# Half of the first feed-forward pair's first matrix moved into the last four attention steps

## The chip, the cores and the metric

The kernel runs on one core of a Trainium2 chip. The metric is the device time of one execution in microseconds (us), lower is better. Five engines work side by side, each with its own instructions in a fixed order: TensorE (PE: matmuls; PEld is its loading of weights), VectorE (DVE), ScalarE (ACT), GpSimd (POOL), and SyncE (SP), which here issues nearly all DMA transfers. An engine goes to its next instruction only when the one before has been released by the semaphores that it waits for, so a waiting instruction holds up everything behind it on its engine. The profile also shows the clock that was granted to TensorE, as a share of full speed (PEclk).

## The reference

One layer on 16 sequences of 128 queries of width 512, all in fp32, in three parts. Each adds its result to its input `x`:

```python
x = x + cross_attention(layernorm(x), ctx)   # 16 heads of 32, context of 2048 positions for each sequence
x = x + mamba_block(layernorm(x))
x = x + ffn(layernorm(x))                    # shared matrix + two gated experts' share, width 512 to 512

def mamba_block(Z):
    x, z = split(Z @ in_proj.T)                          # 2 x 1024 channels
    x = silu(causal_conv(x))                             # four taps along the 128 positions
    dt, B, C = split(x @ x_proj.T)
    h[t] = exp(dt * A) * h[t-1] + dt * B * x             # 16 states for each channel: the scan
    y = (sum_n h[t] * C + x * D) * silu(z)
    Zm = rmsnorm(y @ out_proj.T + Z) * norm1_w
    h1 = gelu(Zm @ w1.T + b1)                            # 512 -> 2048
    return rmsnorm(h1 @ w2.T + b2 + Zm) * norm1_w        # 2048 -> 512
```

The change bears on `Zm` and on `h1` of the first two sequences.

## The kernel before

**Attention.** The loop `for u in range(last)` near line 1160 is the backbone. For u from 0 to NU − 1 = 255 it is an attention step: one sequence, one block of 512 context positions, one group of four heads. A step goes on PE as `scores(u)` (L302, four matmuls into the four PSUM banks), `weighted(u-1)` (L346, the values of the step before, into the PSUM tile `avp`), and `turn(u, i)` (L333, 16 transposes of the exponentials). Between scores and turn lie `maxima(u)` on DVE (L310, four reductions of the banks) and `exps(u)` on ACT (L320, four exponentials). `turn` copies its banks to the tiles `pT` on ACT (L338), one in four on DVE (L336). PE also makes keys and values from the context in these steps (L240), as products of sums of blocks with prepared factors of the weights: tiles `ka..` and `ks..` hold those for the keys. That work, `y_products` and `x_products`, uses the PSUM tiles `pa` and `pc`. Its last part is in step 252. In steps 253 to 255 PE has attention alone, and in step 256 only `weighted(255)`.

**Mamba.** The sequences form 8 groups of two. Group g runs behind attention: its scans, step r of 32, lie in step u = 54 + 32g + r. `decays` (L664, ACT) write exp(dt·A) of four of 16 states into a state buffer in PSUM, one half (i = 0, 1) after the other, `scan` (L678, DVE) runs the recurrence in place, L681 multiplies with C, and POOL adds up (L694). `inputs` (L643, POOL) prepare the next step's right side `w`. The rows `bc` with B and C are loaded by SP (L592) for every step, two loads of 512 KB, each of which waits for the instruction that last read its buffer. The state buffer is `hst`; for the second half, `states` (L651) names `pc` instead from step NU − 2 = 254 on, when `pc` is no longer needed for keys and values. `anew` sets the first position of a state buffer to zero (a memset, L657).

**Feed-forward.** Pairs of sequences m = 0 to 7, 256 tokens each: `z_norm(m)` is the RMS norm of two sequences (a root in small steps on DVE and ACT, lines 73 to 91, then two products of 128 × 512, L806), `turned_in` and `turned_pair` turn the rows (L813, L834) into a tile `mT`, `hidden(m, q)` multiplies with a quarter q of `w1` (L842: four chunks of 128 columns, each four matmuls over 256 tokens, which the profile counts as 32 instructions a quarter), `gelus(m, q)` (L856) writes `hs` with a table load of ACT before and one after, `second(m, q)` multiplies with a quarter of `w2` (L873), and further units hold the experts and the sums. A quarter of `w1` or `w2` is loaded by `load_wf` into two tiles `wf` of 512 KB (six buffers).

**The order.** It is written out by hand. Dictionaries (`late`, `after`, `inner`, `middle`, `loads`, `head`, `behind`) put functions at places inside a step u: `loads` at its start, `middle` after the second scan, `late` after that on PE (transposes and projections, each given a PSUM bank), `inner` near its end. From step NU + 1 = 257 on, the list `units` of the feed-forward part is fed into the steps evenly: `feeds * (u - NU) // (last - 1 - NU)` units up to step u, with last = 314. `feed(k)` issues the loads of unit k + 2, PE's work of unit k, and what comes after unit k − 1. At u = NU the attention pool is closed, PSUM banks go to a free list, and `open_ffn` opens the feed-forward pool, turns the pair's copies into `mT`, loads `b1` and the first two quarters of `w1`. For pair 0, the rows come by `load_z(0)` in step 251, `z_norm(0)` in step 253, its transposes in step 255.

Of the kernel before, what the change touches and what calls it, by code (L numbers as in the profile page):

```python
# [15 lines left out]
P = 128  # L16
# [18 lines left out]
def perceiver_layer(ctx: ExitStack, tc: tile.TileContext, a: dict, out: bass.AP):  # L35
# [73 lines left out]
    with ExitStack() as es:  # L109
# [8 lines left out]
        def acon_in(name, shape, src=None):  # L118
            t = acon.tile(shape, FP, tag=name, name=name)
            nc.gpsimd.dma_start(t, a[name] if src is None else src)  # L120
            return t
# [364 lines left out]
        dtb = acon_in("dtb", [P, EC])  # L486
        dskip = acon_in("dskip", [P, EC])
        aneg = acon_in("alog", [P, EC, DS])

        zTs, xas, zss, bcs, dts, wts, ysum, wts_in = ({} for _ in range(8))  # L490
        sgs = []
# [158 lines left out]

        def states(g, r, i):  # L651

            return pc if i and 32 * (g + 1) + LAG + r >= NU - 2 else hst

        def anew(h):

# [71 lines left out]
        def open_ffn():  # L728
            p = es.enter_context(tc.tile_pool(name="ffn", bufs=1))
            fpool.append(p)  # L730

            def put_in(name, src, shape):
                t = p.tile(shape, FP, tag=name, name=name)
                nc.sync.dma_start(t, src)
                fcs[name] = t

            turned_pair(0)
            load_wf(0, 1, 0)
            put_in("b1", a["b1"], [P, FC])
            load_wf(0, 1, 1)  # L740

        def load_rows():
            for name in ("b2", "fbias"):
# [57 lines left out]
        def z_norm(m):  # L801
# [3 lines left out]
            for i, b in seqs(m):  # L805
                nc.vector.scalar_tensor_tensor(  # L806
                    xrs[b], xrs[b], r[:, i : i + 1], fcs["normw"], ALU.mult, ALU.mult
                )

        def turned_in(src, b, key, ps=None):  # L810
            ps = bank() if ps is None else ps
            for kc in range(KC):
                nc.tensor.transpose(heads(ps)[:, kc, :], src[:, kc * P : (kc + 1) * P], ident)  # L813
            stage[b, key] = ps
# [22 lines left out]
        def hidden(m, q):  # L837
            ps = [bank(), bank()]
            for j in range(4):
                w = wfs[m, 1, q, j // 2]  # L840
                for kc in range(KC):
                    nc.tensor.matmul(  # L842
                        ps[j // 2][:, j % 2 * MT : (j % 2 + 1) * MT],
                        w[:, kc, j % 2 * P : (j % 2 + 1) * P],
                        mTs[m][:, kc, :],
                        start=(kc == 0),
                        stop=(kc == KC - 1),
                    )
            stage[m, q] = ps

        def gelus(m, q):
            ps = stage.pop((m, q))
            t = fpool[0].tile([P, 4, MT], FP, tag="hs", name=f"hs{m}_{q}", bufs=4)
            for j in range(4):
                fc = q * 4 + j
                nc.scalar.activation(  # L856
                    t[:, j, :],
                    ps[j // 2][:, j % 2 * MT : (j % 2 + 1) * MT],
                    AF.Gelu,
                    bias=fcs["b1"][:, fc : fc + 1],  # L860
                )
            nc.scalar.preload_act_table_set("natural_log_exp_and_others")
            give_back(*ps)
            hss[m, q] = t

        def second(m, q):
            if q == 0:
                accs[m] = [bank(), bank()]
            order = [(j, i) for j in range(4) for i in range(MB)]
            if q == 3:  # L870
                order.sort(key=lambda ji: ji[1])
            for j, i in order:
                nc.tensor.matmul(  # L873
                    accs[m][i],
                    hss[m, q][:, j, i * NQ : (i + 1) * NQ],
                    wfs[m, 2, q, j // 2][:, j % 2, :],
                    start=(q == 0 and j == 0),
                    stop=(q == 3 and j == 3),
                )
# [129 lines left out]
        both = tuple(range(MB))  # L1009

        def hidden_units(m):
            for q in range(4):
                unit([call(load_wf, m, 1, q)], [call(hidden, m, q)], [call(gelus, m, q)])
            if m:
                units[-4][2].append(call(mlp_norm, m - 1, both))
                units[-3][2].append(call(last_norm, m - 1, both))
                units[-1][1].insert(0, call(x_turned, m - 1, both))
# [58 lines left out]
            )  # L1076


        late, after, inner, middle, loads, head, behind = ({} for _ in range(7))

        def put(where, u, f):
            where.setdefault(u, []).append(f)
# [45 lines left out]

        for b in range(1, B):
            put(late, 16 * b - 6, lambda ps, b=b: turned(b, ps))  # L1130
        put(inner, NU - 3, lambda: anew(pc))
        put(loads, NU - 20, load_normw)
        put(loads, NU - 5, lambda: load_z(0))
        put(inner, NU - 3, lambda: z_norm(0))
        for i, b in seqs(0):
            put(late, NU - 1, lambda ps, b=b: turned_in(xrs[b], b, "mT", ps))


        ways = (("k", pa, pc, "u2"), ("v", halves(banks[0]), halves(banks[1]), "u2v"))
# [56 lines left out]
        for u in range(last):  # L1196
            live = u < NU
            g, r = divmod(u - 32 - LAG, 32)
            scans = 0 <= g < NG

            made, phase = divmod(u + 3, 4)
            makes = 0 < made < B * SB
            of, phase = ("k", "v")[phase // 2], phase % 2
            load_bc(u + 2 - 32 - LAG, 0)
            if u % 4 == 1 and made + 1 < B * SB:
                load_ctx(made + 1, ("c00", "c10", "c11"))
            if u % 4 == 2 and made + 1 < B * SB:
                load_ctx(made + 1, ("c01",))
            for f in loads.get(u, ()):
                f()  # L1210
            if scans:
                decays(g, r, 0)
            if u > NU:
                while fed < feeds * (u - NU) // (last - 1 - NU):
                    feed(fed)
                    fed += 1
            load_bc(u + 1 - 32 - LAG, DS)
            if u == NU + 1:
                load_rows()
            if live:  # L1220
                scores(u)
            if 1 <= u <= NU:
                weighted(u - 1)
            if u == NU:
                att.close()
                give_back(flat(pa), banks[2], banks[1], flat(avp))
                open_ffn()
            if u == NU + 8:
                load_wex()
            for f in head.get(u, ()):  # L1230
                f()
            if live:
                maxima(u)
            if makes:
                x_products(of, made, phase, pa, pc)
            if live:
                exps(u)
            if makes and u % 4 == 1:
                ctx_sums(made, ("t1", "t2"))
            if 0 <= u + 1 - 32 - LAG < 32 * NG:  # L1240
                inputs(*divmod(u + 1 - 32 - LAG, 32))
            if makes and u % 4 == 1:
                ctx_sums(made, ("t3", "t4"))
            silu_third()
            if scans:
                scan(g, r, 0)
            if makes:
                hold(of, made, pa, "u1")
            if scans:
                decays(g, r, 1)  # L1250
            if makes:
                x_sums(of, made, phase, pa, pc)

            after_turns = late.get(u, ())
            places = [banks[(3 + i) % 4] for i in range(len(after_turns))]
            if live and after_turns:
                if u % 4 == 0:
                    places = [flat(avp), *places[:-1]]  # L1260
                elif u % 2 and makes and u not in behind:
                    places[-1] = flat(pc)
            taken = sum(any(p is b for b in banks) for p in places)
            if live:
                for i in range(3 if taken else 4):
                    turn(u, i, i)
            if scans:
                scan(g, r, 1)
            for f in middle.get(u, ()):
# [99 lines left out]
```

## Time and profile before

| | us |
|---|---|
| median of three runs | 3802.73 |
| lowest and highest run | 3801.78, 3805.72 |
| the profiled execution's own time | 3809.03 |
| its span, from the first to the last instruction | 3807.2 |
| PE busy in the span | 3747.0 |
| DVE, ACT, POOL busy | 2690.4, 2443.9, 2107.1 |
| `scores` of steps 252, 253, 254, 255 begin at | 3069.46, 3080.39, 3087.69, 3101.64 |
| `weighted(255)`, first `hidden`, first `second` begin at | 3111.93, 3118.39, 3151.33 |

Busy time of an engine is the union of its instructions; idle time of one that isn't the bound costs nothing. In a timeline row the first number is the start, the second the length of a run of equal instructions, and the bracket says how long the engine stood idle before it and which instruction ended that by the record of semaphores. A wait for several semaphores is put down to the last. Times inside the execution are from the start of its span.

### The profile page before, as it was taken

What the parts mean: (1) busy time and instruction counts of PE and PEld (TensorE: products, weight loads), DVE (VectorE), ACT (ScalarE), POOL (GpSimd) and SP (SyncE); (2) the same over time, 40 slices, a digit from 0 to 9 for tenths busy, and PEclk for the clock granted to TensorE, in tenths of its full rate; (3) what the DMA queues carried; (4) which work ended last, traced back from release to release, by engine and by line L of the source; (5) the groups of instructions that cost most, each with busy time, mean ns of one, the idle gap of its engine ahead of it and who ended that gap; (6) DMA issues with size and microseconds to landing.
All of it is one profiled execution on the core that took longest, in us unless ns stands there. A gap on an engine that the chain in (4) does not pass through costs nothing.

```text
span 3807.2 us, 70317 instructions
## 1 busy us (share of the span) xinstructions
PE 3747.0 (98%) x26120; PEld 2858.7 (75%) x26120; DVE 2690.4 (71%) x4852; ACT 2443.9 (64%) x5847; POOL 2107.1 (55%) x1968
## 2 busy tenths in 40 slices
PE   8999999999999999999999999999999989999999
PEld 7878787778777877787778878787878766655555
DVE  3444445887878777877787778877887777767843
ACT  3555556777767776777677767776777665545421
POOL 2111213675667665766676566666676667567730
PEclk9999999999999999999999999999999989999999
DMA  3111122444444435353534353445344457577752
GB/s 101 34 40 43 55 65 79 136 154 139 137 162 141 156 120 176 129 166 118 175 131 156 116 187 128 148 134 178 131 148 136 159 186 263 191 256 257 263 194 72
DMA packets 341223, 548.40 MB, mean 144 GB/s; under 512 B 24432, under 2 KB 225408, under 8 KB 340624
## 3 DMA queue, kind: packets, MB, share of 16 engines
q1 hardware_dynamic: 340464, 543.28, 43.2%
q8 instruction: 206, 3.38, 0.4%
q14 instruction: 137, 1.12, 0.1%
q0 software_dynamic: 416, 0.63, 0.1%
HBM read 527.29 MB, written 16.52 MB: 143 GB/s over the span
## 4 chain that ended last, share of the span: by engine, by line
PE 90%; DVE 5%; ACT 3%; issue 1%; POOL 1%; DMA 1%; SPq 0%; DVEq 0%; POOLq 0%; ACTq 0%
PE pa L240 24%; PE pc L240 17%; PE bank L333 11%; PE bank L302 7%; PE avp L346 6%; PE bank L526 4%; PE bank L873 3%; PE bank L968 2%; PE bank L842 2%; PE bank L472 2%; PE avp L399 1%; PE bank L707 1%; PE pc L707 1%; PE pa L873 1%; PE pc L526 1%
## 5 line engine op out<-in xcount | busy, mean ns | idle before, releaser
L310 DVE TENSOR_REDUCE nm<-bank 128x1 f32<-128x512 f32 x1024 | 635.3, 682 | 250.2 <-PE bank L302 250.0
L694 POOL TENSOR_TENSOR ysum<-ysum,w 128x512 f32<-128x512 f32 x384 | 500.7, 1304 | 487.7 <-DVE hst L657 305.8
L320 ACT ACTIVATE pr<-bank,nm 128x512 f32<-128x512 f32 x1024 | 689.8, 687 | 101.0 <-DVE nm L310 97.0
L643 POOL TENSOR_TENSOR w<-dx,bc 128x512 f32<-128x512 f32 x512 | 653.0, 1296 | 4.7
L678 DVE TENSOR_TENSOR_SCAN hst<-hst,w 128x512 f32<-128x512 f32 x456 | 557.0, 1221 | 12.8 <-ACT hst L664 8.5
L338 ACT COPY pT<-bank 128x512 f32<-128x512 f32 x816 | 434.9, 585 | 183.2 <-PE bank L333 179.4
L333 PE MATMUL bank<-ident,pr 128*128 128x128 f32 x4096 | 517.5, 274 | 14.4 <-ACT pr L320 10.5
L664 ACT ACTIVATE hst<-dt,alog 128x254 f32<-128x254 f32 x912 | 436.5, 479 | 145.5 <-DVE hst L657 126.1
L333 PEld LDWEIGHTS bank<-ident,pr 128*128 128x128 f32 x4096 | 471.4, 142 | 66.1 <-ACT pr L320 17.0
L346 PEld LDWEIGHTS avp<-pT,v 128*32 128x32 f32 x8192 | 208.6, 110 | 195.0 <-issue 177.4
L681 DVE TENSOR_TENSOR w<-hst,bc 128x512 f32<-128x512 f32 x456 | 315.2, 691 | 21.2 <-DMA bc<-bcd 5.7
L232 POOL TENSOR_TENSOR t<-c,c 128x512 f32<-128x512 f32 x128 | 164.4, 1285 | 259.4 <-PE pc L240 253.2
L302 PE MATMUL bank<-kt,qT 32*128 32x512 f32 x2048 | 301.3, 643 | 0.9 <-ACT pT L338 0.9
L346 PE MATMUL avp<-pT,v 128*32 128x128 f32 x8192 | 277.6, 276 | 0.0
L240 PE MATMUL pa<-t,ks 128*128 128x256 f32 x1024 | 249.8, 387 | 6.1 <-POOL t L232 6.1
L240 PE MATMUL pa<-vs,t 128*128 128x256 f32 x1008 | 244.7, 386 | 0.0
L240 PEld LDWEIGHTS pa<-t,ks 128*128 128x128 f32 x1024 | 184.8, 190 | 44.2 <-issue 10.6
L240 PEld LDWEIGHTS pa<-vs,t 128*128 128x128 f32 x1008 | 185.4, 190 | 34.6 <-issue 10.1
L320 ACT ACTIVATION_READ_ACCUMULATOR pr<-bank,nm 128x1 f32 x1024 | 209.9, 205 | 0.0
L336 DVE COPY pT<-bank 128x512 f32<-128x512 f32 x208 | 143.8, 691 | 89.6 <-PE bank L333 88.1
L232 POOL TENSOR_TENSOR t<-c,t 128x512 f32<-128x512 f32 x128 | 163.4, 1276 | 36.5 <-issue 19.6
L526 PE MATMUL bank<-zT,win 128*128 128x256 f32 x792 | 182.7, 381 | 0.0
(319 smaller groups left out, 6890.4 us busy)
## 6 DMA issues: line engine op xcount, KB each, us to landing
bc<-bcd SPq DMA_DIRECT2D x512, 512.0 KB, 4.3
c<-in_ctxT_dram SPq DMA_DIRECT2D x256, 256.0 KB, 4.3
wf<-in_w_dram SPq DMA_DIRECT2D x128, 512.0 KB, 7.0
wqo<-in_wqkvo_dram SPq DMA_DIRECT2D x128, 256.0 KB, 4.9
win<-in_win_dram SPq DMA_DIRECT2D x128, 256.0 KB, 4.5
wout<-in_wout_dram SPq DMA_DIRECT2D x128, 256.0 KB, 4.0
x<-in_x_dram SPq DMA_DIRECT2D x16, 256.0 KB, 4.3
x1d<-x SPq DMA_DIRECT2D x16, 256.0 KB, 2.1
```

Of the source, the lines that this page charges most:

```text
L240: nc.tensor.matmul(ps[:, r, :], l[:, kc, r * P : (r + 1) * P], m[:, kc, :], start=(i in (1, 2, 5) and r == 0 and kc == 0), stop=(r == 1 an ...
L302: nc.tensor.matmul(banks[j], qts[b][rows, hg, :], kts[u // 4, hg][rows, :], start=True, stop=True)
L310: nc.vector.tensor_reduce(stats[b][0][j][:, sb, hg : hg + 1], banks[j], AX.X, ALU.max, negate=True)
L320: nc.scalar.activation(pr[:, j, :], banks[j], AF.Exp, bias=nm[j][:, sb, hg : hg + 1], accum_out=sm[:, sb, h : h + 1],)
L333: nc.tensor.transpose(ps[:, j, :], prs[u][:, j, i * P : (i + 1) * P], ident)
L338: nc.scalar.copy(pT, ps)
L346: nc.tensor.matmul(avp[j * HD : (j + 1) * HD, hg, :], vts[u // 4, hg // 2, i // 2][:, i % 2, hg % 2 * P + j * HD : hg % 2 * P + (j + 1) * HD],
L526: nc.tensor.matmul(ps, w[:, kc, :], zTs[g][:, kc, :], start=(kc == 0), stop=(kc == KC - 1))
L643: nc.gpsimd.tensor_tensor(w, dx.unsqueeze(1).to_broadcast([P, NH // 2, GT]), bcs[g * 32 + r, 0][:, i * NH // 2 : (i + 1) * NH // 2, :], AL ...
L664: nc.scalar.activation(bt(h[:, k, :])[:, :, 1:], bt(dt)[:, :, 1:], AF.Exp, scale=aneg[:, ec, n : n + 1],)
L678: nc.vector.tensor_tensor_scan(flat, flat, w.rearrange("p n t -> p (n t)"), 0.0, ALU.mult, ALU.add)
L694: nc.gpsimd.tensor_tensor(s, s, w, ALU.add)
```

## The change

- `b1` is loaded at the start, by the queue of the other constants, not in `open_ffn`.
- The rows of pair 0 are loaded in step 249, not 251. Their norm is cut into `early_first` (step 248), `early_second` and `early_third` (249), and `early_norm` of each sequence (250, 251). `early_turned` transposes both in step 252, and copies them in halves into two tiles of the tag `ws`, which Mamba's weights use.
- The first half of `w1`, quarters 0 and 1, is loaded in eight chunks of 256 KB: four in step 251 into the tiles of factors of keys that are no longer used, four in step 252 into tiles of the tag `ws`.
- `early_hidden` multiplies two chunks in each of steps 253 to 256, in `pa`, `pc`, `pa`, `pc`, between `weighted(u-1)` and the turns of the step. `early_gelus` follow at the end of steps 254 and 256, into tiles of the tag `zs`.
- As `pa` and `pc` are taken, `states` gives `pc` to the second half only from step 257 on, and its first memset is in step 256.
- `hidden_units(0)` has two units, not four; `open_ffn` loads quarters 2 and 3. The feed of units into steps 257 to 313 is spread over 65 units, not 67. `hss` holds four separate tiles or slices for each quarter.

```diff
-            return pc if i and 32 * (g + 1) + LAG + r >= NU - 2 else hst
+            return pc if i and 32 * (g + 1) + LAG + r > NU else hst
...
-            turned_pair(0)
-            load_wf(0, 1, 0)
-            put_in("b1", a["b1"], [P, FC])
-            load_wf(0, 1, 1)
+            load_wf(0, 1, 2)
+            load_wf(0, 1, 3)
...
+        def early_first():
+            ms, r = small("ms", [P, MB]), small("rz", [P, MB])
+            mean_square(keep, ms, mvz[:, 0:MB, :])
+            stage["early"] = r, *root_first(keep, ms, 1e-6)
+
+        def early_second():
+            root_second(*stage["early"][1:])
+
+        def early_third():
+            root_third(*stage["early"])
+
+        def early_norm(i):
+            x = xrs[i]
+            nc.vector.scalar_tensor_tensor(
+                x, x, stage["early"][0][:, i : i + 1], fcs["normw"], ALU.mult, ALU.mult
+            )
+
+        def early_turned(i, ps):
...
+            for kc in range(KC):
+                nc.tensor.transpose(heads(ps)[:, kc, :], xrs[i][:, kc * P : (kc + 1) * P], ident)
+            for h in range(2):
+                copy = nc.vector.tensor_copy if i else nc.scalar.copy
+                copy(mTs[0][h][:, :, i * NQ : (i + 1) * NQ], heads(ps)[:, 2 * h : 2 * h + 2, :])
+
+        def load_early(c):
+            if c < 4:
+                tag = ("ka11", "ka12", "ks3", "ka22")[c]
+                t = pool.tile([P, 2, 256], FP, tag=tag, name=f"w1_{c}", bufs=1)
+                t = t.rearrange("p a b -> p (a b)").rearrange("p (k o) -> p k o", o=P)
+            else:
+                t = ssm.tile([P, KC, P], FP, tag="ws", name=f"w1_{c}", bufs=WS)
+            nc.sync.dma_start(t, a["w1"][c // 4][:, :, c % 4 * P : (c % 4 + 1) * P])
+            wfs["early", c] = t
+
+        def early_hidden(c):
+            ps = (pa, pc)[c // 2 % 2][:, c % 2, :]
+            for kc in range(KC):
+                nc.tensor.matmul(
+                    ps,
+                    wfs["early", c][:, kc, :],
+                    mTs[0][kc // 2][:, kc % 2, :],
+                    start=(kc == 0),
+                    stop=(kc == KC - 1),
+                )
+
+        def early_gelus(q):
+            hss[0, q] = [ssm.tile([P, GT], FP, tag="zs", name=f"hs0_{q}_{j}", bufs=16) for j in range(4)]
+            for j in range(4):
...
+                    (pa, pc)[j // 2][:, j % 2, :],
+                    AF.Gelu,
+                    bias=b1[:, fc : fc + 1],
...
+            nc.scalar.preload_act_table_set("natural_log_exp_and_others")
...
-            for q in range(4):
+            for q in range(0 if m else 2, 4):
...
-        put(inner, NU - 3, lambda: anew(pc))
-        put(loads, NU - 5, lambda: load_z(0))
-        put(inner, NU - 3, lambda: z_norm(0))
-        for i, b in seqs(0):
-            put(late, NU - 1, lambda ps, b=b: turned_in(xrs[b], b, "mT", ps))
+        put(loads, NU - 7, lambda: load_z(0))
+        put(inner, NU - 8, early_first)
+        put(middle, NU - 7, early_second)
+        put(inner, NU - 7, early_third)
+        for i in range(MB):
+            put(inner, NU - 6 + i, lambda i=i: early_norm(i))
+            put(late, NU - 4, lambda ps, i=i: early_turned(i, ps))
+        for c in range(8):
+            put(loads, NU - 5 + c // 4, lambda c=c: load_early(c))
+            put(early, NU - 3 + c // 2, lambda c=c: early_hidden(c))
+        put(inner, NU - 2, lambda: early_gelus(0))
+        put(inner, NU, lambda: early_gelus(1))
+        put(inner, NU, lambda: anew(pc))
+        put(inner, NU, lambda: give_back(flat(pa)))
...
-                give_back(flat(pa), banks[2], banks[1], flat(avp))
+                give_back(*banks, flat(avp))
                 open_ffn()
+            for f in early.get(u, ()):
+                f()
```

More of the change, by code (lines that the diff above doesn't have):

```diff
@@ L488, in perceiver_layer @@
         aneg = acon_in("alog", [P, EC, DS])
+        b1 = acon_in("b1", [P, FC])
         zTs, xas, zss, bcs, dts, wts, ysum, wts_in = ({} for _ in range(8))
@@ L730, in open_ffn @@
             fpool.append(p)
[L732 to L735, printed above, removed]
-            turned_pair(0)
-            load_wf(0, 1, 0)
-            put_in("b1", a["b1"], [P, FC])
-            load_wf(0, 1, 1)
+            load_wf(0, 1, 2)
+            load_wf(0, 1, 3)
         def load_rows():
@@ new lines, in early_turned @@
+        def early_turned(i, ps):
+            if i == 0:
+                mTs[0] = [
+                    ssm.tile([P, KC, P], FP, tag="ws", name=f"mT0_{h}", bufs=WS).rearrange(
+                        "p a b -> p (a b)"
+                    ).rearrange("p (k t) -> p k t", t=MT)
+                    for h in range(2)
+                ]
+            for kc in range(KC):
[3 more added lines that the diff above has]
+                copy(mTs[0][h][:, :, i * NQ : (i + 1) * NQ], heads(ps)[:, 2 * h : 2 * h + 2, :])
@@ L810, in turned_in @@
+        def early_gelus(q):
+            hss[0, q] = [ssm.tile([P, GT], FP, tag="zs", name=f"hs0_{q}_{j}", bufs=16) for j in range(4)]
+            for j in range(4):
+                fc = q * 4 + j
+                nc.scalar.activation(
+                    hss[0, q][j],
+                    (pa, pc)[j // 2][:, j % 2, :],
+                    AF.Gelu,
+                    bias=b1[:, fc : fc + 1],
+                )
+            nc.scalar.preload_act_table_set("natural_log_exp_and_others")
         def turned_in(src, b, key, ps=None):
@@ L844, in hidden @@
                         w[:, kc, j % 2 * P : (j % 2 + 1) * P],
-                        mTs[m][:, kc, :],
+                        mTs[m][:, kc, :] if m else mTs[m][kc // 2][:, kc % 2, :],
                         start=(kc == 0),
@@ L859, in gelus @@
                     AF.Gelu,
-                    bias=fcs["b1"][:, fc : fc + 1],
+                    bias=b1[:, fc : fc + 1],
                 )
@@ L863, in gelus @@
             give_back(*ps)
-            hss[m, q] = t
+            hss[m, q] = [t[:, j, :] for j in range(4)]
         def second(m, q):
@@ L874, in second @@
                     accs[m][i],
-                    hss[m, q][:, j, i * NQ : (i + 1) * NQ],
+                    hss[m, q][j][:, i * NQ : (i + 1) * NQ],
                     wfs[m, 2, q, j // 2][:, j % 2, :],
@@ L1076, in perceiver_layer @@
             )
+        early = {}
         late, after, inner, middle, loads, head, behind = ({} for _ in range(7))
```

## The prediction

> **What bounds the kernel now.** First the page's rows of busy time and of granted clock, and its chain of the work that ended last:
>
> ```profile
> PE 3747.0 (98%) x26120; PEld 2858.7 (75%) x26120; DVE 2690.4 (71%) x4852; ACT 2443.9 (64%) x5847; POOL 2107.1 (55%) x1968
> ...
> PEclk9999999999999999999999999999999989999999
> ...
> PE 90%; DVE 5%; ACT 3%; issue 1%; POOL 1%; DMA 1%; SPq 0%; DVEq 0%; POOLq 0%; ACTq 0%
> ```
>
> TensorE (PE) is busy 98% of 3807.2 us, so most of the kernel gains nothing from a freer VectorE (DVE) or ScalarE (ACT). But one digit of the clock row is an 8, where attention hands over to the feed-forward part: the place of the change. So second the stretches from step 253 on (columns: window, its length, busy time and count of PE, PEld, DVE, ACT, POOL, then granted clock, DMA share, GB/s). The cuts are the starts of steps 253, 254, 255, of `weighted(255)`, and of the first `hidden` matmul:
>
> ```profile
> 3080.39:3087.69 7.30, 4.79 (x58) 2.95 (x57) 5.55 (x9) 5.75 (x15) 6.27 (x7) 1.00 0.31 118
> 3087.69:3101.64 13.95, 7.49 (x57) 4.87 (x57) 11.70 (x24) 7.17 (x19) 6.78 (x6) 0.72 0.25 88
> 3101.64:3111.93 10.29, 10.13 (x67) 7.20 (x66) 8.57 (x14) 6.49 (x16) 5.03 (x4) 0.55 0.30 104
> 3111.93:3118.39 6.46, 1.08 (x33) 0.84 (x33) 5.96 (x12) 5.04 (x12) 5.27 (x5) 0.95 0.70 219
> 3118.39:3125.00 6.61, 6.61 (x17) 5.30 (x18) 6.31 (x13) 3.18 (x6) 5.50 (x7) 0.53 1.07 364
> 3125.00:3150.00 25.00, 25.00 (x119) 21.98 (x118) 13.20 (x22) 18.50 (x35) 21.18 (x22) 1.00 1.03 389
> ```
>
> Read PE's time against the length: from 3080.39 to 3118.39 it works 23.5 of 38 us, and part of that at half clock. After 3125 it is full again, with DMA nearly full too. Third, PE's timeline names the gaps (start, length, instruction; in brackets the idle time before it and who ended it):
>
> ```profile
> 3096.67 0.47 PE L333 MATMUL bank<-ident,pr 128*128 128x128 f32 x1 [5.88 <-ACT pr L320]
> ...
> 3109.29 1.85 PE L813 MATMUL bank<-ident,xr 128*128 128x128 f32 x8
> ...
> 3118.39 6.75 PE L842 MATMUL pa<-mT,wf 128*128 128x256 f32 x16 [5.38 <-ACT hst L664]
> 3124.98 7.07 PE L842 MATMUL bank<-mT,wf 128*128 128x256 f32 x32
> ```
>
> The 5.88 us wait for `exps(254)`. Behind it stands the order of DVE, from its timeline and SP's:
>
> ```profile
> 3092.35 2.85 DVE L806 SCALAR_TENSOR_TENSOR xr<-xr,rz,normw 128x512 f32<-128x512 f32 x2
> 3095.12 2.47 DVE L310 TENSOR_REDUCE nm<-bank 128x1 f32<-128x512 f32 x4
> ...
> 3113.12 1.23 SPq L774 DMA_DIRECT2D wf<-in_w_dram  x2
> ```
>
> `z_norm(0)`, 3089.22 to 3095.2 on DVE, sits ahead of `maxima(254)`, whose scores were ready by 3089.8. The 5.38 us are put down to an ACT instruction that writes no operand of the matmul. I take the weights as the releaser: issued at 3113.12, and their tile's fastest landing in this stretch is 5.1 us, hence 3118.2. Sixteen hidden instructions then take 6.75 us where the next 32 take 7.07 (3.46 for 16): 3.3 us lost to the clock.
>
> **The change, part by part.** I follow PE from 3080.39 to the end of `hidden` of pair 0. In the profile that is 3150.02, less 0.87 for six small instructions of lines 459 and 610 in between (3142.25 to 3143.12): 3149.15, or 68.8 us.
>
> *Norm in parts.* The 6.0 us of DVE leave step 253. `early_first` is 0.27+0.27+0.90 = 1.4 us, `early_third` 1.25, the two products 1.43 each, now in steps 248 to 251. There PE is full (steps 250 to 252 take 10.9, 9.6 and 10.9 us with no bracket on PE, DVE 9.2 of 10.9 busy in step 252), and the products with key and value factors hide them; without that cover they would cost their 5.5 us. Value 0; the stall it removes is counted below.
>
> *Transposes.* The eight of line 813 leave step 255 (1.85 us at half clock) and go to step 252 at 0.88 us (8 × 0.11, as in the row of L333). The four half copies on ACT and DVE fall under the factor products of step 252. So step 253 starts at 3081.3.
>
> *Early matmuls.* Eight chunks of four matmuls, which the profile counts as 64 instructions: 64 × 0.216 (7.07 us for 32, by their spacing 6.91) = 13.8 us, two chunks (3.46 us) in each of steps 253 to 256, between `weighted(u-1)` and `turn(u)`. Step by step, at full clock (scores 1.07, weighted 1.07, turn 16 × 0.11 = 1.75):
> - 253: scores and weighted to 3083.4, chunks 0, 1 to 3086.9; `exps(253)` are done by then (they ended near 3085 in the trace), turn to 3088.6.
> - 254: scores to 3089.7, weighted to 3090.8, chunks 2, 3 to 3094.2, turn to 3096.1. `maxima` and `exps` (2.5 and 2.8 us) lie under the chunks.
> - 255: the first scores wait some 0.9 us for a copy as they do at 3087.69, to 3098.4; weighted to 3099.4; chunks 4, 5 wait about 0.9 for `early_gelus(0)` to free `pa`, to 3103.7; turn waits for `exps(255)`.
> - Those `exps` stand behind `early_gelus(0)` on ACT: a table load of 1.28, four of 0.42, a load of 1.28, 4.2 us. By ACT's order they run 3103.3 to 3106.0, so turn ends at 3107.6, line 610 at 3108.1, `weighted(255)` at 3109.2. In the trace it ended at 3113.0.
> - 256: chunks 6, 7 to 3112.65.
>
> *`states`.* Both halves of the scans of 254 to 256 use one buffer, so `decays` of the second half wait for the first scan: 0.7 to 1 us on ACT in each, as in all steps up to 253 today. It is inside the ACT order above; alone it could cost 0 to 3 us. `anew(pc)`, a memset of 0.06 us, moves to 256.
>
> *What is left of `hidden`.* q = 2 and 3. Their tiles wait for the attention pool, for a copy of step 255, and on SP behind a `bc` load that waits for the second scan of 255 (about 3109.8): issued near 3110.3, landing 5.1 us later, 3115.4. PE waits 2.75 us. Then 64 instructions, 13.8 us: 3129.2. If the tile takes the 7.3 us that is the median of these loads in 3108 to 3165, the wait is 4.95.
>
> *Eight added loads* of 256 KB in steps 251 and 252, in a stretch at 0.31 of DMA's share; 4.3 us is what loads of that size take, and 10 us pass before use. On SP two of them wait for factor products of step 250. Behind them is queued a `bc` load that then goes out near 3060.4 and is used near 3074: slack of 9 us after landing. `b1` at the start, 8 KB: nothing.
>
> Sum: 3149.15 − 3129.2 = 19.95 us. Its parts: 3.8 from `weighted(255)` ending earlier although 10.4 us of hidden work now stand before it; 2.6 less wait for weights (5.38 to 2.75); 3.3 of clock; 13.8 hidden matmuls that no longer follow; less 3.45 for chunks 6, 7 before the wait. That is 20.05, within rounding.
>
> *After it.* From 3118 on PE waits for only some 26 us in 690, so a lead of PE reaches the end as far as the others keep pace. DVE has 42.97 of 50 us in 3450 to 3500, and the pace rises by 20/690 = 3%: enough. (The loop now spreads 65 units over the same steps, not 67; each step still holds some 8 us of PE units.) But at some points PE comes close to others: `second(0, 0)` needs `w2` tiles that are issued by step, the adds of POOL at 3153.9 (line 467), `wex`. I take off 2 us for such waits (bounds 0 and 8): **18 us**.
>
> Two rules bear on this. First, the row: ACT's gelu load starts at 3123.98 after an instruction that ended at 3123.96, and lasts 1.28; no other gap stands around it. The Trainium skill, "ScalarE: Activation LUTs", section "What ACT_TABLE_LOAD costs", puts 1.38 us of drain on top of each switch: 2.66 in all. By it `early_gelus(0)` would hold ACT for 7.0 us, and `exps(255)` end 2.8 us later: gain 15. The row decides, 18. Second, the clock: the gaps of 5.88 and 5.38 us were each followed by 0.5. "TensorE: Matmul & The Clock Gate", Part 1, names an idle window of about 3.4 us. My wait of 2.75 lies below it, so the clock stays at 1.0; at 4.95 it would not, and the gain falls by 2.2+3.3 to 12.5. The trace has no gap between 0.93 and 5.38 here, so the edge is the page's.
>
> **Rivals.**
> *It pays less (gain 4 to 12, about 3795).* The weights land late and the clock drops (−5.5), and the one-buffer scans and gelus each push ACT by 2 to 3 us. For it: DMA moves 364 to 389 GB/s after 3118, its share 1.03 and above. Against it: two of the four MB of `w1` are in before.
> *Slower.* The loads of `w2` stay tied to the steps while PE is 20 us ahead. In the trace they go out from 3133.56 for use at 3151.33; now use is at 3130. I get 3.5 MB ahead of and with the first, 3110.3 + 9.5 + 2 = 3122, and 7 MB up to the second, 3131 for use at 3137: slack of 6. If each of the four units found its tile over 3.4 us late, each costs that and 3.3 of clock: 4 × 6.7 = 27 us, 9 over the gain, **3812**. Up to 2.7 us late it remains a gain of 7 or more.
> *More (gain 24 to 28).* SP frees earlier, so that the wait for weights vanishes (2.75), and two waits of the tail, 4.6 us for ACT ahead of line 526 and 3.4 for POOL ahead of line 580, close as PE's other work falls differently beside them: 3774 to 3779.
> *It doesn't do it:* the early matmuls could merely lengthen the attention steps by their own 13.8 us, as they would if scores and copies, not `exps`, paced them. Then only the norm's stall is won, about 5 us: 3798, part of the first rival.
>
> **How the numbers follow.** The runs' median is 3802.73, the profiled execution 3809.03 with a span of 3807.2; the sum uses differences inside that span, which I take off the median: 3802.73 − 18 = **3785**. Chances: this 0.58 (own range 3780 to 3791), less 0.19, more 0.13, giving the gain back 0.10, of which 0.07 ends slower. A difference under 0.2% (7.6 us: 3795.1 and 3810.3) can't be told from none. Half of the "less" case lies beyond it: faster 0.58 + 0.13 + 0.09 = 0.80; same 0.10 + 0.03 = 0.13; slower 0.07. For 8 in 10 the range drops the slower case and the far end of "more": 3773 to 3801.
>
> **What would show it.** Right: the waits of PE in steps 253 to 256 sum to under 6 us, granted clock 1.00 from step 254 on, `weighted(255)` ends near 3109, the first matmul of q = 2 is preceded by 2 to 3 us, `second(0, 0)` starts near 3130, and PE's idle time after it stays near 26 us. Wrong: a wait over 3.4 us and clock near 0.5 in 254 to 257 (ACT's gelus or weights), or new waits of `second` for `wf` after 3130, or PE's lead at 3130 present but gone in the tail.

## The result and the profile after

The changed kernel takes 3791.64 us (six runs, 3787.74 to 3794.15) where the kernel before takes 3804.77 beside it (six runs, 3801.78 to 3806.85): ratio 0.9959, 95% interval 0.9949 to 0.9969, so 12 to 19 us less; the two medians lie 13.1 us apart. Two later sets gave 0.9958 and 0.9955. Forecast were 18 us less.

From the page of the changed kernel, the rows of busy time, of granted clock and of the chain that ended last:

```profile
PE 3742.2 (99%) x26120; PEld 2853.8 (75%) x26120; DVE 2689.9 (71%) x4853; ACT 2443.5 (64%) x5848; POOL 2109.4 (56%) x1969
...
PEclk9999999999999999999999999999999999999999
...
PE 89%; DVE 5%; ACT 3%; DMA 1%; issue 1%; POOL 1%; SPq 0%; DVEq 0%; POOLq 0%; ACTq 0%
```

The 8 in the clock row is gone. The stretches that answer to those of before (same columns): steps 253, 254 and 255, `weighted(255)` with chunks 6 and 7, the wait for weights, and the first 3 us of `hidden`:

```profile
3081.84:3089.32 7.48, 7.48 (x74) 5.89 (x73) 4.64 (x8) 5.93 (x15) 5.16 (x5) 1.00 0.24 83
3089.32:3098.17 8.85, 8.31 (x73) 6.64 (x73) 7.50 (x13) 6.29 (x17) 5.93 (x6) 1.00 0.20 61
3098.17:3109.71 11.54, 10.08 (x75) 6.77 (x75) 7.49 (x12) 11.04 (x23) 5.04 (x4) 1.00 0.39 136
3109.71:3114.44 4.73, 4.73 (x49) 3.76 (x48) 4.62 (x10) 2.36 (x5) 3.41 (x4) 1.00 0.46 131
3114.44:3116.93 2.49, 0.00 (x0) 0.03 (x1) 1.25 (x3) 2.02 (x4) 1.92 (x2) 0.97 0.93 310
3116.93:3120.00 3.07, 3.07 (x7) 2.49 (x8) 2.58 (x7) 3.04 (x6) 1.96 (x2) 0.50 1.08 383
```

Steps 253 to 255 keep the full clock, and step 254 is 8.85 us where it was 13.95, with 3.46 us of hidden work in it. But step 255 is 11.54, longer than the 10.29 of before, with ACT busy 11.04 of it. And the wait for weights is still followed by half clock. PE's timeline at the hand-over:

```profile
3101.29 3.72 PE L851 MATMUL pa<-mT,w 128*128 128x256 f32 x16
...
3110.72 3.72 PE L851 MATMUL pc<-mT,w 128*128 128x256 f32 x16
3116.93 15.65 PE L903 MATMUL bank<-mT,wf 128*128 128x256 f32 x64 [2.50 <-DMA wf<-in_w_dram]
3132.42 1.02 PE L934 MATMUL avp<-wf,hs 128*128 128x512 f32 x2
```

The wait of 2.50 us is now put down to the load itself, as was read from the issue time before. The 64 hidden instructions take 15.49 us to the next start; at full clock they would take 13.8.

What one execution can tell: the start of the program alone moves the span by up to 4 us. `scores(250)` begin between 3045.64 and 3049.63 us in the traces of the runs. The clock granted in the first 60 us differs too: in executions of the kernel before, of the changed kernel and of the run `e1_norm` below it was (window row, same columns; PEclk is the third number from the end):

```profile
0.00:60.00 60.00, 50.18 (x256) 39.67 (x257) 22.91 (x42) 17.91 (x42) 18.46 (x25) 0.94 0.45 138
```

```profile
0.00:60.00 60.00, 52.49 (x255) 40.74 (x256) 21.56 (x42) 17.98 (x42) 18.56 (x26) 0.91 0.43 138
```

```profile
0.00:60.00 60.00, 51.59 (x300) 39.95 (x300) 23.07 (x44) 18.82 (x44) 19.00 (x26) 1.00 0.43 138
```

The changed kernel's own three executions have 0.91, 0.97 and 0.97, so the change is not what sets it. `scores(250)` begin at 3048.88, 3049.15 and 3045.93 in the three above. The parts of the norm in steps 248 and 249 lie before that point, but the kernel before and the changed one go through these two steps in 27.44 and 27.45 us. So profiles are compared here from `scores(250)` to the end of the span. For the kernel before that is 3807.2 − 3048.88 = 758.3 us. For the changed kernel, profiled three times, it is 742.9, 743.9 and 745.3: 15.5, 14.5 and 13.0 less. So this measure too is good only to some 2 us.

### The profile page after: what moved, and what is told of

Its sections match the earlier page's. It is cut to its first block, busy times and chain, and to the rows that moved or that the text cites. A ratio compares the mean times of both kernels' runs of the same rounds, so it can differ in the third digit from the quotient of the medians.

```text
span 3792.0 us, 70325 instructions
## 1 busy us (share of the span) xinstructions
PE 3742.2 (99%) x26120; PEld 2853.8 (75%) x26120; DVE 2689.9 (71%) x4853; ACT 2443.5 (64%) x5848; POOL 2109.4 (56%) x1969
## 4 chain that ended last, share of the span: by engine, by line
PE 89%; DVE 5%; ACT 3%; DMA 1%; issue 1%; POOL 1%; SPq 0%; DVEq 0%; POOLq 0%; ACTq 0%
PE pa L240 24%; PE pc L240 17%; PE bank L333 11%; PE bank L302 7%; PE avp L346 6%; PE bank L527 5%; PE bank L1029 2%; PE bank L934 2%; PE bank L472 2%; PE bank L708 2%; PE bank L903 1%; PE avp L399 1%; PE pc L708 1%; PE avp L934 1%; PE pa L934 1%
## 5 line engine op out<-in xcount | busy, mean ns | idle before, releaser
L679 DVE TENSOR_TENSOR_SCAN hst<-hst,w 128x512 f32<-128x512 f32 x459 | 560.7, 1222 | 15.8 <-ACT hst L665 9.3
L333 PEld LDWEIGHTS bank<-ident,pr 128*128 128x128 f32 x4096 | 469.6, 141 | 57.5 <-issue 13.8
L682 DVE TENSOR_TENSOR w<-hst,bc 128x512 f32<-128x512 f32 x459 | 317.4, 692 | 26.0 <-DMA bc<-bcd 10.4
```

The costliest lines, as they stand in the source:

```text
L333: nc.tensor.transpose(ps[:, j, :], prs[u][:, j, i * P : (i + 1) * P], ident)
L679: nc.vector.tensor_tensor_scan(flat, flat, w.rearrange("p n t -> p (n t)"), 0.0, ALU.mult, ALU.add)
```

## The experiments

Ratios are to the kernel before, run beside each. The "lead" is how much earlier than in the kernel before the first `second` matmul starts, counted from `scores(250)`. The 2.18 us of small matmuls of lines 459 and 610 that stand ahead of it in the kernel before are taken off where a run has them behind it.

| run | ratio, interval | lead, us | `scores(250)` to end, us | less than before, us |
|---|---|---|---|---|
| changed kernel | 0.9959 (0.9949 to 0.9969) | 17.0 | 742.9 | 15.5 |
| `e1_norm` | 0.9968 (0.9955 to 0.9980) | 7.2 | 748.7 | 9.6 |
| `e2_load` | 0.9957 (0.9945 to 0.9970) | 14.5 | 743.2 | 15.1 |
| `e3_states` | 0.9994 (0.9986 to 1.0002) | 1.0 | 759.4 | −1.1 |
| `e5_q2`, `r_e5` | 0.9952 (0.9939 to 0.9964), 0.9951 (0.9938 to 0.9965) | 21.3, 21.3 | 740.8, 745.8 | 17.5, 12.5 |
| `r_after`, `r_after2` | 0.9958 (0.9945 to 0.9970), 0.9955 (0.9942 to 0.9967) | 16.6, 18.1 | 743.9, 745.3 | 14.5, 13.0 |
| `e6_fill` | 0.9961 (0.9947 to 0.9974) | 18.3 | 742.6 | 15.8 |
| `e7_steps` | 0.9965 (0.9952 to 0.9977) | 14.8 | 743.8 | 14.5 |
| `e8_clock` | 0.9991 (0.9983 to 1.0000) | 5.0 | 753.5 | 4.8 |

### The norm alone

From the changed kernel, the early matmuls and their loads are taken out again:

```diff
-            return pc if i and 32 * (g + 1) + LAG + r > NU else hst
+            return pc if i and 32 * (g + 1) + LAG + r >= NU - 2 else hst
-        for c in range(8):
-            put(loads, NU - 5 + c // 4, lambda c=c: load_early(c))
-            put(early, NU - 3 + c // 2, lambda c=c: early_hidden(c))
-        put(inner, NU - 2, lambda: early_gelus(0))
-        put(inner, NU, lambda: early_gelus(1))
-            for q in range(0 if m else 2, 4):
+            for q in range(4):
```

> This has only the norm in parts, its transposes in step 252 and the copies in halves; all four quarters of hidden stay behind attention, weights loaded as before. Theory (the norm's place in VectorE's order made the 5.88 us gap, and the half clock after it): steps 253 to 255 take about 7.5 us each, weighted(255) ends near 3105 instead of 3113, the wait for the first weights stays over 5 us with half clock after it; 8 us faster than before, ratio 0.998. Rival (the gap is filled by other waits of the exponentials, and most of the change's 15 us comes from the matmuls put into gaps): 2 to 4 us faster, ratio 0.999 to 0.9995.

Measured: 0.9968, and 9.6 us by the profile. Its PE timeline:

```profile
3085.91 2.09 PE L302 MATMUL bank<-kt,qT 32*128 32x512 f32 x8 [0.93 <-ACT pT L338]
...
3093.16 2.10 PE L302 MATMUL bank<-kt,qT 32*128 32x512 f32 x8
...
3109.63 5.35 PE L903 MATMUL pa<-mT,wf 128*128 128x256 f32 x16 [5.89 <-DMA wf<-in_w_dram]
```

Step 254 is 7.25 us (3085.91 to 3093.16), not 13.95: the gap of 5.88 is gone, and no other took its place. The wait for weights stays, at 5.89, with half clock after it. The theory holds: 9.6 of the 13 to 15.5 us at the end are there with 6 us of VectorE work moved out of the way of four reductions. (The eight transposes left step 255 with it, so their share is in this number.)

### The weights early, the matmuls behind attention

To `e1_norm`, the eight chunks are loaded in steps 252 and 253 (four into two context tags kept in a pool of their own, four into `ws`), and `hidden(0, 0)` and `hidden(0, 1)` use them as ordinary units after attention:

```diff
+        for c in range(8):
+            put(loads, NU - (3 if c < 4 else 4), lambda c=c: load_early(c))
...
-                w = wfs[m, 1, q, j // 2]
+                early = m == 0 and q < 2
+                w = wfs["early", 4 * q + j] if early else wfs[m, 1, q, j // 2]
```

> As the run with the norm alone, and the first half of w1 is loaded in steps 252 and 253, but its matmuls follow attention, none lies in an attention step. Theory (weights at hand remove the 5.4 us wait and the half clock behind it; filling gaps brings only about 1 us on balance, since the changed kernel has a wait of 2.5 us and half clock before q = 2 again): first hidden matmul within 1 us of weighted(255)'s end, clock 1.00, end of hidden near 3133; 15 us faster than before, ratio 0.996, as the changed kernel. Rival (filling the gaps is what pays): no better than the norm alone plus 3, so 5 to 11 us faster.

Measured: 0.9957, 15.1 us by the profile; the changed kernel, which has half of those matmuls in attention's steps, has 13.0 to 15.5. Its first hidden matmul follows `weighted(255)` at once:

```profile
3101.74 1.08 PE L348 MATMUL avp<-pT,v 128*32 128x128 f32 x32
3102.75 3.72 PE L908 MATMUL pa<-mT,w 128*128 128x256 f32 x16
```

So the weights' early arrival is worth the rest, and the place of the matmuls nothing that can be seen at the end. A part of the reason is in the lengths of steps 253, 254 and 255 of this run, against 7.48, 8.85 and 11.54 in the changed kernel:

```profile
3078.53:3085.83 7.30, 4.78 (x58) 2.94 (x57) 5.55 (x9) 5.75 (x15) 5.16 (x5) 1.00 0.37 128
3085.83:3093.27 7.44, 6.05 (x56) 3.75 (x56) 6.47 (x13) 6.56 (x17) 5.59 (x6) 0.94 0.20 73
3093.27:3101.74 8.47, 7.93 (x59) 4.94 (x59) 7.67 (x13) 6.77 (x17) 5.35 (x5) 0.65 0.52 183
```

In the changed kernel the chunks, with the gelus and the one-buffer scans that came with them, lengthen the three steps by 0.2, 1.4 and 3.1 us: 4.7 of the chunks' own 10.4. Of the 5.7 won, 2.5 go to the wait for weights, which this run doesn't have, and 1.7 to the half clock behind it. With nothing but chunks 6 and 7 between `weighted(255)` and quarter 2, the loads that wait for attention's end have lost their cover. `e2_load` in turn loses about 1 us, most of it in a wait of 0.93 us for POOL within `hidden`. So the matmuls in the gaps do bring some 2.5 us, the difference of the two leads, 17.0 and 14.5. At the end it is gone: the other part of the reason lies behind the hand-over, and `e6_fill` below shows it.

### One buffer for the scans

```diff
-            return pc if i and 32 * (g + 1) + LAG + r >= NU - 2 else hst
+            return pc if i and 32 * (g + 1) + LAG + r > NU else hst
...
-        put(inner, NU - 3, lambda: anew(pc))
+        put(inner, NU, lambda: anew(pc))
```

> The kernel before with one edit: both halves of the scans of steps 254 to 256 use one buffer. Theory (decays then wait for the first half's scan, as in all steps up to 253): 0 to 2 us slower, ratio 1.000 to 1.0005. Rival (the second buffer had hidden more): 3 to 6 us slower.

Measured: 0.9994, interval 0.9986 to 1.0002, and 1.1 us more by the profile. No cost of 3 us or more; the first answer stands.

### Filling the idle time with matmuls that nobody reads

Three runs put matmuls of identity by the norm's weights, 128 x 512, into PE's gaps, to see what the half clock costs by itself:

```diff
+        def idle_fill(n, ps):
+            for i in range(n):
+                nc.tensor.matmul(ps, ident, fcs["normw"], start=True, stop=True)
...
+            if u in (NU - 2, NU):
+                idle_fill(6, flat(pa))
```

The first is the kernel before with six of them behind `weighted` in steps 254 and 256, as in the diff:

> The kernel before, with six matmuls that nothing reads (5.2 us) in each of its two long gaps: before the turns of step 254, and before the first hidden matmul. Nothing is moved. Theory (of the time before, some 7 us are not the waits themselves but the half clock after each): turns of 254 at full speed (1.5 us), step 255 some 2.5 to 3 us shorter, the first 16 hidden instructions 3.3 us shorter, sum 6 to 8 us faster, ratio 0.998. Rival (PE at half clock was still ahead of the exponentials, so only the hidden matmuls gain): 3 to 4 us.

Measured: 0.9991 (0 to 6.5 us), 4.8 by the profile. The clock stayed at 1.00 from 3078 to 3124, while the exponentials and the weights came no earlier. The first hidden instructions after the filled gap:

```profile
3108.07 5.42 PE L1081 MATMUL pa<-normw,ident 128*128 128x512 f32 x12
3114.50 3.69 PE L842 MATMUL pa<-mT,wf 128*128 128x256 f32 x16 [1.01 <-ACT pc L664]
```

3.69 us where it was 6.75, as expected. Step 254 fell from 13.95 to 12.77 us (3085.70 to 3098.47) and 255 from 10.29 to 8.59. Together 1.2 + 1.7 + 3.1 = 6.0; but the first `hidden` matmul came 7.44 us after the start of `weighted(255)`, not 6.46, which leaves 5.0 at this place, and 4.8 at the end. It lies between the two expectations: in the attention steps the exponentials hide a part of the half clock.

The same in the changed kernel, three matmuls at the hand-over:

```diff
+            if u == NU:
+                idle_fill(3, banks[0])
```

> The changed kernel with three matmuls added that nothing reads (identity by the norm's weights, 128 x 512, some 2.6 us in all) in the 2.5 us in which PE waits for the tile of quarter 2. Theory (the wait, though only 2.5 us long, makes the clock fall to half for 3.2 us): the first 16 hidden instructions take 3.5 us and not 5.1, granted clock 1.00 throughout, 1.6 us faster than the changed kernel. Rival (the half clock comes from the crowded DMA or the reload of work after the hand-over, not from idle time): half clock stays, no gain, or 0.1 us lost.

```profile
3110.77 2.74 PE L1142 MATMUL bank<-normw,ident 128*128 128x512 f32 x6
3113.70 14.05 PE L903 MATMUL bank<-mT,wf 128*128 128x256 f32 x64 [0.19 <-DMA wf<-in_w_dram]
```

14.05 us for the 64 instructions, not 15.65, under the same crowded DMA (its share 1.05 to 1.08 in the first 6 us), so the crowd alone does not halve the clock. That the fill prevented it here is likely, not shown: the changed kernel itself, unfilled, kept full clock at this place in one of three executions (`r_after2`, told at the end). For gaps of over 5 us `e8_clock` shows it.

The ratio is 0.9961, beside 0.9958 for the changed kernel: of a lead 1.3 us longer (18.3 for 17.0) nothing can be seen at the end. The expectation of 1.6 us at the end failed. Where the lead went, the next rows show; the first is of the changed kernel, the second of `e6_fill`, the third of `r_after2`:

```profile
3156.25 0.66 PE L874 MATMUL bank<-ident,xr 128*128 128x128 f32 x4 [0.44 <-DVE xr L800]
...
3152.93 0.66 PE L874 MATMUL bank<-ident,xr 128*128 128x128 f32 x4 [2.34 <-DVE xr L800]
...
3154.88 2.25 PE L874 MATMUL bank<-ident,xr 128*128 128x128 f32 x8 [3.01 <-DVE xr L800]
```

PE turns the rows of pair 1, and waits for VectorE's norm of that pair. That norm comes no earlier with a longer lead (its products start 105.1, 105.8 and 107.3 us after `scores(250)`), so the wait grows, and in the last two the clock then falls to half for 3.4 us. From the first `second` matmul to the one after these turns and eight more matmuls (L934 at 3160.18, 3159.55 and 3161.09), PE takes 27.8, 32.0 and 32.2 us: a lead of over 18 us is back below that of the changed kernel.

And in the three steps of `e2_load`, two such matmuls each:

```diff
+            if NU - 3 <= u < NU:
+                idle_fill(2, flat(pa))
```

> As the run with the norm and the early weights, whose matmuls follow attention, and in steps 253, 254 and 255 two matmuls that nothing reads between weighted and turn (1.7 us a step, inside the wait for the exponentials). Theory (in that run the clock fell to half at 3092 although no gap there was over 0.93 us, because two steps in a row were only 65 to 77% busy; useful work in the gaps pays mostly by keeping the clock): clock 1.00 from 3078 on, weighted(255) ends some 3 us earlier, 2 to 3 us faster than that run, so 17 to 18 us faster than before. Rival (each gap is too short to matter and the half clock there has another cause): clock falls again, 0 to 1 us slower than that run.

Measured: 0.9965, and 14.5 us by the profile, against 15.1: no gain. The clock was 1.00 throughout, as expected, yet the steps stayed as they were:

```profile
3082.32:3089.61 7.29, 6.03 (x61) 3.62 (x61) 5.55 (x9) 5.75 (x15) 5.17 (x5) 1.00 0.37 123
3089.61:3096.86 7.25, 6.98 (x61) 4.17 (x61) 6.28 (x12) 6.37 (x17) 5.39 (x6) 1.00 0.23 75
3096.86:3105.23 8.37, 7.62 (x63) 4.49 (x63) 7.79 (x13) 6.89 (x17) 5.57 (x5) 1.00 0.54 178
```

22.9 us for the three, 23.2 without the fill. The theory fell here: the half clock in `e2_load`, from 3092.4 to 3099.2, cost almost nothing. In step 255 the exponentials start 2.84 us after the scores in both runs (3096.11 and 3099.70 on ACT), since VectorE's scan and maxima, not the scores, hold them up. It is not so wherever it falls: in `e1_norm` half clock from 3099.3 to 3102.7 met the last turns and line 611, with nothing else to wait for, and step 255 took 9.47 us instead of 8.37.

### A quarter more

To the changed kernel, quarter 2 is loaded in step 253 as well, into context tags in a pool that stays open, and multiplied right behind chunks 6 and 7:

```diff
+                for c in range(8, 12):
+                    early_hidden(c)
+                stage[0, 2] = banks[0:2]
                 att.close()
-                give_back(*banks, flat(avp))
+                give_back(*banks[2:], flat(avp))
...
+        for c in range(8, 12):
+            put(loads, NU - 3, lambda c=c: load_early(c))
...
-            load_wf(0, 1, 2)
             load_wf(0, 1, 3)
+            load_wf(0, 2, 0)
```

> The changed kernel, and quarter 2 of w1 is loaded in step 253 too, into two context tiles kept in a pool of their own, and multiplied right behind chunks 6 and 7, into the first two banks; the loads at the hand-over are quarter 3 and the first of w2. Theory (the 2.5 us wait before q = 2 and the half clock of 3.2 us after it, 1.6 us lost, are all that is left there): no gap at the hand-over, clock 1.00, 4 us faster than the changed kernel, so about 19 us faster than before, ratio 0.995. Rival (the loads of w2 or the tail take it back): the same as the changed kernel, ratio 0.996, with new waits of second for its tiles or for the gelus.

```profile
3109.87 3.72 PE L860 MATMUL pc<-mT,w 128*128 128x256 f32 x16
3113.43 7.07 PE L860 MATMUL bank<-mT,w 128*128 128x256 f32 x32
3120.33 7.07 PE L912 MATMUL bank<-mT,wf 128*128 128x256 f32 x32
3127.24 1.02 PE L943 MATMUL avp<-wf,hs 128*128 128x512 f32 x2
...
3153.79 0.63 PE L461 MATMUL bank<-ident,fx 128*128 128x128 f32 x4 [3.17 <-DVE avs L468]
3154.25 5.29 PE L943 MATMUL avp<-wf,hs 128*128 128x512 f32 x8
```

No gap at the hand-over, no half clock; `second(0, 0)` starts 4.3 us earlier than in the changed kernel (3127.24 to 3132.42, less the 0.86 by which `scores(250)` differ). Its lead is 21.3 us. Then PE waits 3.17 us for VectorE, and eight matmuls take 5.29 us instead of 3.60. VectorE's timeline just before that:

```profile
3138.96 0.69 DVE L684 TENSOR_TENSOR w<-hst,bc 128x512 f32<-128x512 f32 x1 [1.97 <-DMA bc<-bcd]
...
3145.48 3.16 DVE L804 SCALAR_TENSOR_TENSOR xr<-xr,rz,normw 128x512 f32<-128x512 f32 x2
3148.57 1.22 DVE L681 TENSOR_TENSOR_SCAN hst<-hst,w 128x512 f32<-128x512 f32 x1
```

It is the first picture once more: `z_norm(1)` of the next pair, whole, ahead of the scans and the product that frees PE's bank, and a late `bc` load before it.

> The kernel with quarter 2 early too, measured beside the changed kernel. Theory (its lead of 4 us at the hand-over is half eaten by waits of TensorE for VectorE in the tail, as its first trace shows): 2 us faster than the changed kernel. Rival (all of it is eaten): 0.

> The changed kernel beside the next one on one chip: 0.9958 to 0.996 of before.

Medians beside each other: 3789.70 and 3791.90, of before 0.9951 and 0.9955. The intervals overlap, and by the profiles it is 17.5 and 12.5 us against 13.0 to 15.5, so a gain over the changed kernel is possible, not shown.

> The changed kernel once more, beside the others of this set on one chip. Expected 0.996 of before, 13 to 16 us, as measured first; the three others are compared with it.

Measured 0.9958. Its profile and that of `r_after2` have a use of their own, told at the end.

## Why the prediction was right, and where not

**The bound and the two gaps.** Right. The norm ahead of `maxima(254)` was the cause of the 5.88 us (`e1_norm`), and the loads of the 5.38 us: `e1_norm` and the changed kernel name them, and with the weights at hand (`e2_load`) the wait is gone.

**Norm in parts at no cost, transposes 0.88.** Right: steps 248 and 249 take as long as before, and step 253 starts at 3081.84, of which 0.27 were there at `scores(250)`; forecast was 3081.3.

**The steps.** 7.48, 8.85 and 11.54 us measured. By the forecast's own times 7.3, 8.5 and 11. `weighted(255)` ended at 3110.7 and not 3109.2; without the 0.27, 1.2 us late. ACT set step 255, as forecast, and without the 1.38 us of drain:

```profile
3099.11 1.28 ACT L863 ACT_TABLE_LOAD   x1
3100.40 0.84 ACT L863 ACTIVATE hs<-pa,b 128x256 f32<-128x256 f32 x2
...
3101.99 1.28 ACT L869 ACT_TABLE_LOAD   x1
3103.28 0.99 ACT L665 ACTIVATE hst<-dt,alog 128x254 f32<-128x254 f32 x2
3104.20 0.67 ACT L320 ACTIVATE pr<-bank,nm 128x512 f32<-128x512 f32 x1
```

The next instruction starts 1.29 us after each load began. The row was a better guide than the 2.66 us of the Trainium skill, "ScalarE: Activation LUTs", section "What ACT_TABLE_LOAD costs". But the forecast let `exps(255)` follow the second load at 3103.3, and left out `decays`, which stand between: 0.92 us, to 3104.20. Line 611 then waited 0.42 for a copy on VectorE. These two are the lag.

**The wait for weights.** 2.75 us forecast, 2.50 measured (2.81 and 2.96 in the other two executions).

**The clock after it.** The step that failed: "My wait of 2.75 lies below it, so the clock stays at 1.0". It fell to 0.50 for 3.4 us and cost 15.49 − 13.8 = 1.7 us. In the sum, 3.3 us of clock were booked as won, and half of that came back. (The 3.3 sets a length, 6.75, against a spacing, 3.46; spacing against spacing it is 6.59 − 3.46 = 3.1.) The trace of before could have warned: farther on, a wait of 2.77 us was followed by half clock too.

```profile
3567.56 1.31 PE L813 MATMUL bank<-ident,xf 128*128 128x128 f32 x8 [2.77 <-DVE xf L921]
...
3568.32:3571.73 3.41, 3.41 (x12) 2.78 (x10) 3.13 (x5) 3.32 (x7) 3.41 (x4) 0.50 0.06 23
```

**The end.** The lead at the end of `hidden` of pair 0 was forecast as 19.95 and is 3149.15 − 3132.42 + 0.27 = 17.0. The tail took 1.5 of it (15.5 at the end); 2 was set down. So 18 becomes 15 by two terms of the sum: 1.2 in step 255, 1.7 of clock. That the tail's term fits is in part luck: in the other two executions it took 2.1 of 16.6 and 5.1 of 18.1. PE's idle time after the first `second` matmul is 27.0, near the 26 that was forecast, and 28.6 in both others. The measured time, 3791.64, lies in the range; of the likeliest case's own range, 3780 to 3791, it misses the edge, partly because the forecast was taken off a median of 3802.73 while the runs beside it gave 3804.77.

**What the sum did not say.** It was right in size, and incomplete as an account of what pays. It booked 13.8 us for matmuls "that no longer follow". `e2_load` has all of them following, and is as fast. By the leads, the norm's place brings 7.2 us, the weights' early load 7.3 and the matmuls in the gaps 2.5. At the end it is 9.6, 5.5 and nothing that can be seen: after the hand-over PE waits less where its lead is short and more where it is long. The rival that "it doesn't do it" thus holds for 4.7 of the 10.4 us in the steps.

**The rivals.** *Slower* did not happen: no `second` waited for a tile of `w2`; after 3132 the only wait in the next 25 us is 0.44 for the norm of pair 1 (1.24 + 0.48 and 3.01 in the other two executions). *More* did not, though the wait of 4.6 us ahead of the rows of L526 did shrink to 0.2. *Less* was near in mechanism (clock lost, ACT late) and not in size.

## What to carry to other kernels

Before work is put into a matmul engine's idle time, ask what made it idle: here a few small vector instructions in the wrong place of an in-order queue were more than half of what was left at the end, and a load that came early the rest. Work that is pulled ahead of a hand-over was also cover for the loads that can start only there; reckon the wait that comes back. And a lead at one place is spent at the next engine that keeps its own pace: of 4.3 us and of 1.3 us more at the hand-over, at most some 2 and none were left at the end, because PE soon waited for VectorE.

## What was not expected of the hardware

A wait of less than 3 us can halve TensorE's clock, or leave it. Three executions of the same changed kernel, at the same wait; the first, of 2.50 us, is above, with clock 0.50 after it. The next is `r_after`, the last `r_after2`:

```profile
3113.13:3115.94 2.81, 0.00 (x1) 0.03 (x1) 1.53 (x4) 2.35 (x4) 1.91 (x2) 1.00 0.92 306
3115.94:3119.00 3.06, 3.06 (x8) 2.49 (x9) 2.29 (x6) 3.03 (x6) 2.20 (x3) 0.57 1.09 387
```

```profile
3112.07:3115.03 2.96, 0.00 (x0) 0.03 (x1) 1.68 (x4) 2.48 (x4) 1.91 (x2) 1.00 0.97 297
3115.03:3120.00 4.97, 4.97 (x23) 4.40 (x24) 3.06 (x7) 4.86 (x11) 4.09 (x5) 1.00 1.07 397
```

After 2.50 and 2.81 us the clock was 0.50 to 0.57 for 3 us; after 2.96 us it was 1.00. So the length of the gap alone does not decide. That fits a window that runs freely, as the Trainium skill, "TensorE: Matmul & The Clock Gate", has it in Part 1, but here a window need not be wholly idle to count.

The traces show its edges. Read from narrow windows, the stretches at half clock around the hand-over last 3.41 us (changed kernel, `r_after`), 6.83 (`e2_load`) or 17.07 (before, 3093.87 to 3110.94), always a multiple of 3.41. Within one execution the edges lie on one grid: in `r_after` the clock falls at 3116.36, 0.42 us after the wait is over, and again at 3157.32, twelve times 3.413 us later. Before the fall in the changed kernel PE was busy in 1.08 of 3.41 us (3113.36 to 3116.77). In `r_after2`, counted back from its next fall at 3154.98, the wait of 2.96 us is cut by an edge at 3114.02, and the clock stays:

```profile
3110.60:3114.02 3.42, 1.47 (x7) 0.95 (x5) 2.14 (x4) 1.48 (x4) 3.38 (x3) 1.00 0.85 242
3114.02:3117.43 3.41, 2.40 (x11) 2.17 (x12) 3.12 (x7) 3.38 (x6) 1.76 (x2) 1.00 1.05 361
```

Nor is a single gap needed. In `e2_load` no gap of PE in steps 253 and 254 was over 0.93 us, but PE was busy only 4.78 of 7.30 us in the first and in short pieces in the second, and from 3092.4 on the clock was at half for 6.8 us; in `e7_steps`, at 83% in step 253 and more after it, it stayed full. It looks like a matter of the busy share of a window. But PE's busy time as the profile counts it doesn't settle it: of these two windows of `e2_load`, as busy as each other, only the second was followed by half clock.

```profile
3082.15:3085.56 3.41, 2.06 (x15) 1.54 (x14) 2.83 (x6) 2.31 (x7) 1.69 (x2) 1.00 0.47 155
3088.98:3092.39 3.41, 2.07 (x13) 1.51 (x14) 2.75 (x5) 3.38 (x11) 3.25 (x5) 1.00 0.27 101
```

What is counted stays open. And half clock on an engine that waits for others in each step cost 0.3 us of 23 there: the clock matters where PE is the bound, as behind the hand-over.
